# Attention scores of the second layer: computed once with queries on partitions, instead of twice

## The chip, the cores and the metric

The program runs on one core of a Trainium2 chip, in one launch. The metric is the device time of one execution in microseconds. The kernel before was run 23 times: median 2198.99 us, 2188.61 to 2218.9. All intermediate data stay on the device; the host only lays inputs out.

## The reference, cut to what matters

The model is two post-norm layers on 16 sequences of 512 tokens of width 128. Each layer is an attention and a mixture of experts. The change lies in the second attention, which has 16 heads of 8 dimensions and a bias that depends on the distance of query and key alone:

```python
rel = abs(r[None, :] - r[:, None]) / max(S - 1, 1)
idx = clip(round(rel * (RES - 1)), 0, RES - 1)
pos_bias = einsum('ijf,hf->hij', table[idx], Wpos)
q, k, v = split(einsum('bsd,ed->bse', x, Wqkv), 3)      # 16 heads of 8
logits = einsum('bihd,bjhd->bhij', q, k) * scale + pos_bias[None]
attn = softmax(logits, axis=-1)
out = einsum('bhij,bjhd->bihd', attn, v)
return einsum('bsd,ed->bse', out, Wout)
# around it: x = layernorm(x + first_attention(x)); x = layernorm(x + experts(x))
#            x = layernorm(x + this(x));            x = layernorm(x + swiglu_experts(x))
```

The softmax runs over the keys j. A stable softmax takes the row maximum over j from the logits of each query i before the exponential.

## The kernel before, in words

**Order of the work.** The program is written as a list of operations. Each has an engine, a cost, a due time, the buffers that it reads and writes, and a function that emits its instructions. The order in which they are emitted is a table of ranks, `ORDER`, one pair of characters for each operation, made ahead of time. It fixes the order of the instructions on each engine, with SP's transfers and POOL's among them. A tile framework adds the waits. At run time each engine takes its queue in that order, and stands when an operand or a buffer is not ready.

**Buffers.** Pools rotate. The ones that matter: `pair`, three PSUM buffers of 128 x 1024 f32; `one`, two PSUM buffers of 128 x 512 f32; `wide`, twelve SBUF buffers of 128 x 1024 f32. `pair` and `one` together are all of PSUM, and the other stages (the first attention, the experts) draw from the same pools.

**Stages.** The 16 sequences go through in chunks of 2, 3, 4, 3, 3 and 1. While a chunk is in its second layer, the next chunk is in its first, and the experts of the last one run too; the order mixes them closely.

**The second attention of one sequence** (`attention1`). Queries and keys are projected (L1208, L1209) and split into a rounded part `hi` and a rest `lo`, so that four products of rounded numbers make one exact enough score. They go through DRAM (`parts`, L1248) to be spread over partitions (`spread`, L1285). The 16 heads are taken in four groups of four; of a group the four tiles of 128 tokens are taken in turn, and heads in two pairs. For every group there are two passes over the scores:

- *The maxima* (`maxima`). A second copy of queries and keys, rounded to bf16, goes its own way through DRAM (`rounds`, L1259, and four small transfers a group into `qk16_pad`, L1272). For a tile of 128 queries and a pair of heads TensorE adds the bias into PSUM by a product with a bf16 identity (L1308) and the rounded scores on top (L1317): queries on partitions, 512 keys along the row. ScalarE casts the result to bf16 in SBUF (L1333). VectorE folds halves and quarters of the rows by maximum (L1349, L1365, L1376), reduces the rest (L1377) and keeps the negated maximum of each query in `tops`. TensorE turns `tops` (L1392), ScalarE copies it (L1400), and a transfer puts it as one more row beside the queries (L1405, `shift`). The maximum needs no exactness, since it only shifts the exponent.
- *The weights* (`weighted`). For a tile of 128 keys and a pair of heads TensorE forms the scores the other way round (L1422): keys on partitions, 512 queries along the row, with the shift row taken in by a key row of ones (L1858 sets it). VectorE adds the bias out of PSUM (L1441), ScalarE takes the exponential of 1024 columns at once (L1447). The result has keys on partitions, as the product with the values needs it: TensorE adds the four heads' values, weighted, into 4 x 32 rows of `av` (L1456), over the four key tiles. A ninth column of ones in `vaug` gives the sum of the weights.

`normalised` copies `av` (L1467), turns it (L1471) and divides (L1477, L1478). The maxima of a group are due 1.5 tiles before the weights of the group before it (`EARLY`).

The other lines that the prediction uses: L1073, where the first attention turns a tile of 128 x 1024 in eight transposes, and L1076, which copies it to SBUF; L1050, the running sums of the first attention; L1062, L1524, L1234, sums and products on VectorE that read PSUM; L618 and L620, the statistics of a layer norm; L636, its scaling on ScalarE with a scale and a bias of each row; L1143, the experts' activation with a bias of each row; L1223, a scaled copy out of PSUM.

Of the kernel before, what the change touches and what calls it, by code (L numbers as in the profile page):

```python
# [19 lines left out]
P = 128  # L20
# [34 lines left out]
    "#$###M#O#)#N#<#'#(#/#2#6#%#*#3#9#:#5#.#7#?#G#1#,#A#B#H#=#>#T#U#V#W#Y#@#-#P#R#X#4#&#S#b#l#;#+#_#j"  # L55
    "#m#8#Q#d#h#k#`#n#p#q#u#v#z#|#f#K#t$2$:#x#y%]$5$K#e#C#E#F#g#J#0&1%c#D#{$%#L#[#]#^#~$#$$#c#o$)$($0"
    "$*$,$/$4$=$D#i$&$-$6$9$;$<$>$?$H$I$a$1$3$B$C$F$M$G$N$S$T$g$l$@$A$O$P$W$[$]$^$_$o$t$u%-%.%2%7%Y%j"
    "#a#w#I$L$Q$R$U$Y$b$V$X$e$Z$c$f$p$v$z${%($`$d$q$s$y$~$|$}%$%*%4%@$w$x%#%&%'%3%/%1%8%9%I%L%%%)%0%:"
    "%;%=%>%B%C%M%N%S%Z%_%`%d%h%l%m%o%p%s%t&-&_&d'D&C&:&E&N&Q&V&`&b'K&T&m&X&^&x&}'$'*'b&R'9'1'2'?'@'N"
    "'U'd'H'a'W'_'n'o'u'v'w'~(8(:(<(>)*)A)Q)r+A#Z#r#s#}$'$+$.$7$m$8$i$h&'&%&G'](]$J$E%a&&'[$j%W%e$k&D"  # L60
    "'R0b.S)k%Q(A(B(O(V(F(P(H(I(G(Q({(x(c(Z(R([(t(b(q)c)$)s)H)E)F)K(d)-)0)O)1)2)7),).)4)U)>)@)C)D)I)L"
    ")[)l)()))/):);)=)V*'*(*5*:*<(w(_(u(v)g(z(|)#*X*P*T*b*Y*l*|)R)W)X)`)d)i)m*v*[*]*z*}+(+1)Y)e)f)8)?"
    ")G*%*w*o*p*y*x+'+@)M)S)T)5)6)<)n***r*~+$+-*u+<+E)|*)*/*#*$*,*C*D*F*K*f+#+L+M+R)_)b)a)h+H+7+9+U+D"
    "+C+O+Y+J+P+i*4*7*>)q)u)v*H+=+N+T+W+B+k+s*6*8*E)y)z){*U+?+c+g+r+G+I+t*;*=*?*2*3*9*I*L+0+d+l+|+3+j"
    ",%)})~*+*.*0*1*_*c*d*{+:+X,&,/,C*@*M*-*A,++o,,,6,*+Z+_+u,1,2,;*O*S*W*i*j*n+)+m+q+x,-+n+v,>*Z*^*e"
    "*a*g*h+5+^+w+{,:+y,$,B*k*q*s+%+&+*+++>+z,#,5,9+~,),H+.+4+;+,+2+6+F+Q+[+f+p,.,L,V,Z,P,<,?,b,Q,R,m"
    ",E,J,O,l,N,d,w,f,S,T,U,i,|,~,],[,g,o,c-#-'-,-8->-G-H-V-`-n-u.3.G.H.m/3.M.q.W.Y.u/</=9u,',(,e,k,0"
    ",4,@,3,=,M,A,^,D-D,F,a,W,X,G-j-X-0-]---.-2-+-/-4-@,{-&-),z-$-(-?-7-<-=,p,v,x-A-B,y,}-%,j,q,u-C-E"
    "-b.+.-.>,s-3-1,`-g-Z,n-h.A.C.E.K.D.I.V-L-Q-R-9-:-;-o.B.J.O.].P.a.c-a-d-s-I-M-O-t.Q.b.f.v.[.j.y-J"
    "-T-U-c-e-f-q-y.k.h.i.r.l/4/C-Y-[-_-w-{-}-~.&.4.;.R.T/F/V/b-S-^-W-5/(/*/#/'.z/G/O/^.~/_/g.*...2-k"  # L70
    "-z.#.{/A/J/R/i/I/N/l.7.<.?.%.5.:.n/P/Z/`/q/S/d/r.s.t.x.p.w.}/,/-/h/c/k/u/v/y0$.Z.`.g.^._.e.o/2/9"
    "/E/U/]0(0508./.0.=/)0&0+/n0%/p/z0)0//{020N.|/%/1/.///6/>0.0'000<040B0R/&/0/8/Y/a/e/m/~060E0F0*0;"
    "0`/7/;/?/:/@/D/Q/f0G0J0O0^0K0T0f/H/T/[/j/o/t/|0-010@0A0C0i0t0v0Q0M0P0Z0U0[0j0X0V0W0l0Y0h1$0g0c0k"
    "0~0m0p1%0q0r0u1#0s0w1&1'1*1+1217181>1?1B1H1J1Z1d1j1_1b1e1f1i2q3$;v$n$r%+%,%5%6%<%?%A%D%E%H%T%J%K"
    "%P%^%n&#%F%G%O%U%V%g%b%k%v%x&*&+%R%X%i%q%r%|%u%y&)&0&2&7%}%~&$&(&4&5&8&;&<&>&F&O&z'X'x'y(9(;'6%["
    "%f%w%z%{&.&/&9&,&3&A&6&?&@&H&I&]&q'&&=&B&L&M&W&Y&Z&a&c&h&o&y&J&P&S&[&k&l&r&s&t'#'3';&j&n&p&w&|'%"
    "''')','5'<'='O()(3(7(f(m&U&K&e&f&g&i&{&~&u&v'.'('8'-'/'0'4'I'Q'+'7':'A'B'E'M'P'S'^'`'k'>'C'F'G'V"
    "'g'Z'c'l'm'|(0'T'Y'e'q'z(#($(&(.(1(2(E(J(S(e(g(k(n(~)%)3)9)o)w)x,7,K,r*`+/*m*t+K+S+`+a/M+8+h+b+e"
    ",8,I,Y,h-K-*-6-F-N-i-|.6.9/$+}.F.(.)/5/B/W/X09-P/s/w/x0,030?0H0L0S0x0y1.1/0|1l1n4*4a1:2*2M4&4:1k"
    "2%2'2)1v2#2$2P2h2x3=3>3S3T3Y3]3Z3`3c3m3u9j3G4)44464@4D4A4J4N4^4b7X4S585f5l5u6s5~6+6y7d7m9X4Q8.7q"  # L80
    "7t9b9p9e9i9s:*:.:g;g=C=E?;?IFdI`;j<q=D>0>[?@At/+10112_3&13191<1@1;1F1T1U1[1`1R1S1o1x232m3F3#1g2I"
    "2N2b2<2?2@3'2=2>2J2224272{2E2K2L2Q2V2X3(332Y2Z2[2d2j2t2|34353:3O3P1X1Y1V1W262T2z3e3b3^3h3k3l3p4'"
    "2&2-201q1r1u2C4-3r3y4.4/41482A2B2F1c1p1s2G3i43494E3n4=4F1z1{1|2+21252D2e424;4B4K474H4T292:2;2.2/"
    "282H2f2g3[3_3d4X4_4d2^2]2y2l4<4O4R4>4Z3q3v3w4[4f4j2s2u3%2}2~3)374C4%4(4]4L4W4z2i2p2v3/383@3A4e4U"
    "4c4r4k4t4~3-3.32393B3C3I3J4o4h4u5$4q4w5+2w3*3,30313;3H3K3L3z4,4V5.50542R2U2S2O4x5#4p4y4`4{5'5(4g"
    "4s5:2`2a2c2n2o2r364n4}53595%5)5B3M3N3R3<3V3W3j525,5-565;5?5H3f3g3o3Q3U3X3t3|5&555A5D5*575J3~4#4+"
    "3x3}4$404G4I4i4m4|5K5W5b5I5@5N5Q5M5k5z5T5C5F5t5^5m5{5y5w5x6*5}6,6?5V6$6)6L5_5j6[6]6g6x7#7+7B7C7G"
    "7L7n7x889c9n8:8A8>8H8L8T8];t5>5G6/6B5L5S5P5Z5O5p5h6%64665[6&5`616'7?6~7,7K6N6S6V6D6G6K6k636>6A6-"
    "6<6=6I6X6c6e6R6T6U6z7%6C6F6J6@6E6M6h7&7'7Z7a7r6#625]656Q8C6:678,7w7{83868J8S6u6v6{6m6p6t727~7z8&"
    "8*8'818g6o6q6r6a6f6i7-8N8M8U8Z8R8Y8k7(7*7.6w7)757T7U8d8W8X8w8e8h8}787;7D7$70767E7^7o8$8+8?9%9.97"  # L90
    "6|717/6}9l9k9;9o8P8i8q8u8[8s9,7A7H7O77797:7P8j8o8v9(8n9&9/7b7c7e7F7I7J7f9*8x8y8z929S9_7h7s7y7l7v"
    "7}8)8-8r949@9Y8~9>9`7R7[7j7]7_7`7k80939M9T9t9d9~:&7@7>7<7=9h9m9G9F9w9v9z:$9|:6:C8=8E8K7Q7W7Y8Q:;"
    "9}:(:+:<:G:K9=9H9I9<9E9K9N9{:/:7:9:,:>:L9'9+9-8|9)95969A:I:0:4:Q:J:S:i9O9[9a9L9R9]:#:-:8:@:F:N:u"
    ";1;H:X:U:W:f:Y:`:{:q:Z:^:_:s:t;*:l:|;$;):o:p;8:h;#;(;.:n:};9;<;K;c;d;q<$<%<5<><B<C<J<Z<f<t=#<z=&"
    "='=:=A>.:1:2:V:a:3:::A:O:=:H:B:k:T:c:b:r:~:j;&;l;{;y;B;A;E;J;';+;,;m;/;7;@;-;5;>;b;L;M;R;O;Y;];n"
    ";o;4;6;:;f;s;}<-<6<8<D<I<M:m;W:d:e<e;w;V;P<v<T<]<|<w<}=5;S;X;a;T;U;`;r<x=3=7=9<{=2=Q<#<'<.;?;D;I"
    "<7=/=;=@=U=0=X=p;e;p;|<A<E<L<Q<_=6=<===J=8=?=v<&<)<1</<2<<<X<`<a=*=-=N>&>/>4;Z;u;z;x>(>)=M=O=q=^"
    "=`=|=w=z>1<[<g<h<Y<c<d<l=R=t=x>%=S=c>G<O<S<U<P<R<V<j=s=y={>@>$>D>H<=<G<K=$=)=,=F=G=j>9>:>F=r>+>I"
    "<+<3<;<:<@<F=(=V=f=u=}>,>J>f>g<s<u<r<b>c>;>b>?>P>E>O>e>T>h>n=T=Y=Z=L=P=W=e>B>X>Y>k>C>}>~=>=B=H=g"
    "=l=n>3>r>`>a?&>w?$?*=i=k=o=]=a=d>*>M>K>m>o>t>U>|?+=~>8>A>5>6>>>L>N>Q>^>i>j?2?8?:>v>y>{?/?'?.?3>p"  # L100
    "?0?7?B>q?1?K?)?4?<?G?5?H?L>x?6?9?F?,?J?M?N?S?T?W?X?Y?Z?[?]?c?d?e?f?g?h?~?q?r@)@1@SIf'J'L'f'h'i'j"
    "'p's'r't'{'}(((%(/(4(6(?(K('(*(+(,(@(C(L(M(N(U(s(}(=(D(X(Y(^(r(h(i(l)&)p*G(W(a(j)')J)P)^+V+]-m-v"
    "-x.8.@.L.U.X.d6;(-(5(T(`(o(p)B)N(y)+)t)Z)j)]*&*B*N*R*V,_,t-l-p.$.'.,.N/}0#0I0d*J*Q-r/K0]0a0_0e0z"
    "1)1=1M0=0D0n0o1,15161C1D1P1Q1]1^1t2W2k3+3D/L.1070:0>0{1(1-0}141A1I1K1N1a1h1m3a3s1E1G1L1O1}2,1~2("
    "454?5X5d1w1y3?3{5/5=5<5U5c5g6H6O4M4Y4l5R5a5i5o5q5s6W6j6n84898<8B8G8O4P3E4v515E5Y5e5v5n5r5|6(6.68"
    "6P6Y6Z73746^6_6b6l7M7V7N7S7g7p82856`6d7|8/878;8@8V8_8`8m8t8%8(8D8I8^8b8c8l8p8{9#9$90999:9?9B9C9D"
    "9U9V9^9r:E:R:x9y<y=1;C;=;N;[;~<*<4<9<n;2<?<,<0<k<m<~=%>-<i=4=+=.=I=K=[=_>'<p=b=h=m>#>7><>=>_>2>]"
    ">W>Z>l>s>u>z?->V?#?%?(?=?C?D?E?P?R?a?b?k?m?x@,@]AEC&BiD_EOGFG~CwDRH{J0KB?i?l?w@3?j?n@&A-?oA.@%A@"
    "Ah@BB%B,BNB]B[BbBtC$C/C2B}C@C<CIC^CyCcCpD,D@DAJ%C6G)EtEvGKGbGLGOGeGzH'MmD;H?GnGxHjI,HnHzI-JsJ|L#"
    "F>MDJSJfM_N$M`MbN,N4NPNQN|O2O`OjOkP$Q1P<VwVxWBX*ZXb|QPRbRiUcV#VcY<>d?p?t@$@*?u?z?{?v?y@'@5@V@-@X"  # L110
    "@+@U@N@7@9@pA6@oA#@`@b@d@Z@[@c@e@m@n@{A%A&A)A+@w@zA$@g@j@kA0A1@}A(A*A2A3A7A9A=A>ARAjAx@2@4@8@=Aw"
    "A[@lAyB&A|A~B5B(B8BG@?@@@H@a@f@h@iB;A}B#B9BHBMBU?O@6@C@J@K@P@RB>B6B<BKBABOBV@0@<@E@F@O@^@s@tBIBD"
    "BEBFBLBQBX@D@G@I@L@M@W@Y@u@vAJAoA{B`BeBnA/A,A5A4B{B|B~B^BRB.B7BCBSBWBoB)B+B-B/B1B4B=BTBfBkBlBaBh"
    "BvB$B'B*AeAgAsB2BcBgBqBwBdBmC4AlAmAnA]A^AaB?BJBxBzC%C'C(C+C8AfAiAkAqArAzB3BPBZBrBsC#C:C?CN@y@q@r"
    "@xC*C3C-C1CAC.C7CKCECMCVA:A;A<@|@~A'AUC0CCCDCOC>CGCWAHAKAQAPASAWAYC)CPCXCbC9CHC|ADAGAOA8AAACAVAX"
    "CSC[CjCtCTCUD4AMANATABAFAIAZA_A`B@BBCBDFDVDfD0C{C}D=D1D9DICYD#D&D(CZCgDLDKD'D.D/DSDUDiD:D<DCDMD?"
    "D^DkDmD{D~E'E+E8E:E;EAE]E_EpF&F6F9FUFDFJFVG,G;I&C]C`E0E1CaCfCdChClCqC~DOD7D8CmCnD$D+D6DZDbEDEID>"
    "DEDGDdDgDhDvDXD]DcD[D`DaDeDpDrDuDjDnDoDwDxDBDHDQDDDJDTE)E*E/E=EEEJDYD3D%DPFKDNDWDlEYEVEWE`EZEaF-"
    "E<E?E@D|E(E,EMF,F)F*F+F/F7F:E3E6E7E$E-E.EREfF.F2F=EgF1FEEBEFESE4E5E>ETEwF0FHFRFSF3FQFeEKENEUDqDy"
# [156 lines left out]
def block_kernel(ctx: ExitStack, tc: tile.TileContext, d, out: bass.AP):  # L276
# [900 lines left out]
    def attention1(b, x, at):  # L1177
# [117 lines left out]
        def maxima(g, it, lows):  # L1295
# [60 lines left out]
            if it < 2:  # L1356
                return
# [647 lines left out]
```

## Time and profile before

| | |
|---|---|
| median of 23 runs | 2198.99 us |
| profiled execution | 2203.36 us |
| its span, first to last instruction | 2201.6 us |
| mean granted TensorE clock | 0.961 of full speed |
| busy share of DMA engines, 320 to 2110 us | 0.35 |
| TensorE, VectorE, ScalarE busy, 320 to 2110 us | 1632.5, 1442.4, 1337.1 of 1790 us |

The prediction quotes lines of four kinds. A line of a group has the source line, the engine (PE is TensorE, PEld its weight loads, DVE VectorE, ACT ScalarE, POOL GpSimd, SP the queue of transfers), what is written from what, the shapes and the count; after the bar the time during which one of the group ran, the mean length of one in ns, and after the second bar the idle time of the engine just before them with what ended most of it. A line of the timeline has the start, the length and the operation, with neighbours of a kind merged. A line of waits has who waited for whom, the total, the times and the longest. Matmuls overlap, so a mean length says little of what one more costs.

### The profile page before, as it was taken

Reading aid. Unit: us, or ns where it says so; the run is one execution under the profiler, and the core shown is the slowest. Engines: PE = TensorE matmul, PEld = TensorE weight load, DVE = VectorE, ACT = ScalarE, POOL = GpSimd, SP = SyncE. Lnnn points to the kernel's source line nnn. Section 1 sums busy time; section 2 is a strip of 40 time slices with the busy share of each in tenths; the row PEclk is TensorE's granted clock in tenths of the full one; section 3 lists DMA queues with packets and bytes.
Section 4 is the critical chain, followed back from the end, with each engine's and each line's share of the span. In section 5 each row is a group of like instructions: output and inputs, shape, how many; then the busy total and the mean of one; then the engine's idle time right before and its main releaser. Section 6 shows DMA issues by size and latency. Waiting matters only on the chain. (4 is left out here: it accounts for less than half of the span.)

```text
span 2201.6 us, 32021 instructions
## 1 busy us (share of the span) xinstructions
PE 1957.7 (89%) x11336; PEld 1047.8 (48%) x11437; DVE 1694.5 (77%) x2894; ACT 1496.6 (68%) x2066; POOL 802.6 (36%) x879
## 2 busy tenths in 40 slices
PE   4878899998999898889999998899999799899887
PEld 1555644454455454344545443456455344443365
DVE  7555578797979686878797697979878787878866
ACT  5222468876776676667687788666677678799653
POOL 4335551244222634521333343442422633140343
PEclk9899999999999999989999999999999989999899
DMA  4416143423321442422233523233244434342343
GB/s 116 115 60 178 53 145 109 146 78 113 98 92 56 140 129 92 131 78 81 71 104 100 171 80 113 66 126 89 78 128 140 143 100 143 124 129 90 92 160 107
DMA packets 188579, 240.09 MB, mean 109 GB/s; under 512 B 22148, under 2 KB 132612, under 8 KB 188420
## 3 DMA queue, kind: packets, MB, share of 16 engines
q1 hardware_dynamic: 162868, 149.36, 22.5%
q0 software_dynamic: 25552, 88.68, 13.3%
q8 instruction: 91, 1.49, 0.3%
q14 instruction: 68, 0.56, 0.1%
HBM read 164.50 MB, written 80.42 MB: 111 GB/s over the span
## 5 line engine op out<-in xcount | busy, mean ns | idle before, releaser
L1441 DVE TENSOR_TENSOR p<-st,bias 128x1024 f32<-128x1024 f32 x512 | 606.1, 1218 | 81.4 <-PE st L1422 50.5
L1333 ACT CAST low<-s 128x1024 bf16<-128x1024 f32 x512 | 497.8, 1018 | 148.0 <-PE s L1317 114.1
L1447 ACT ACTIVATE p<-p 128x1024 f32<-128x1024 f32 x512 | 520.3, 1057 | 89.2 <-DVE p L1441 78.7
L796 POOL DMA_INDIRECT ws<-tab,rows x201 | 203.3, 1012 | 419.7 <-DVE yq L1153 172.0
L1308 PE MATMUL s<-bias,ident 128*128 128x512 bf16 x923 | 294.1, 400 | 45.1 <-ACT low L1333 26.5
L1456 PE MATMUL av<-p,vaug 128*32 128x512 f32 x2048 | 272.2, 610 | 5.4 <-ACT p L1447 2.7
L1422 PE MATMUL st<-qk_pad 64*128 64x512 f32 x1024 | 233.5, 490 | 47.4 <-DVE p L1441 22.4
L1034 POOL TENSOR_TENSOR self<-ev,own 128x1024 f32<-128x1024 f32 x64 | 127.0, 1986 | 336.2 <-DVE ev L1028 107.2
L1349 DVE TENSOR_TENSOR low<-low 128x1024 bf16<-128x1024 bf16 x256 | 182.7, 720 | 60.9 <-ACT low L1333 52.1
L1422 PEld LDWEIGHTS st<-qk_pad 64*128 64x128 f32 x1024 | 92.2, 189 | 228.6 <-DVE p L1441 71.7
L1308 PEld LDWEIGHTS <-ident 128*128 128x128 bf16 x1024 | 85.7, 99 | 194.0 <-issue 168.1
L796 POOL DMA_INDIRECT yg<-results,place x124 | 124.4, 1003 | 113.8 <-DMA results<-yq 51.1
L1317 PE MATMUL s<-qk_pad 32*128 32x512 bf16 x1024 | 154.7, 393 | 5.2 <-issue 5.1
L1050 PE MATMUL cum<-ev,tri 128*128 128x512 f32 x256 | 131.9, 641 | 16.1 <-DMA ev<-carry 12.5
L1076 ACT COPY ot<-po 128x1024 f32<-128x1024 f32 x64 | 64.8, 1013 | 111.3 <-PE po L1073 78.5
L1062 DVE TENSOR_TENSOR o<-cum,gg 128x1024 f32<-128x1024 f32 x64 | 78.3, 1223 | 79.5 <-PE cum L1050 36.8
L1081 PE MATMUL y<-ow,ot 128*128 128x128 f32 x1024 | 130.6, 283 | 2.7 <-ACT ot L1076 2.5
L1081 PEld LDWEIGHTS y<-ow,ot 128*128 128x128 f32 x1024 | 123.1, 196 | 18.4 <-issue 12.8
L1015 PE MATMUL pv<-vw,xt 128*128 128x512 f32 x256 | 126.2, 619 | 2.6 <-ACT carry L1057 1.5
L626 POOL TENSOR_SCALAR rs<-mv 128x4 f32<-128x4 f32 x63 | 22.0, 349 | 280.2 <-DVE mv L620 256.2
L1028 DVE TENSOR_TENSOR ev<-pv,ex 128x1024 f32<-128x1024 f32 x64 | 78.2, 1221 | 46.1 <-PE pv L1015 45.8
L1317 PEld LDWEIGHTS <-qk_pad 32*128 32x128 bf16 x1024 | 36.0, 91 | 154.7 <-issue 151.0
(226 smaller groups left out, 3173.9 us busy)
## 6 DMA issues: line engine op xcount, KB each, us to landing
qk_pad<-parts SPq DMA_DIRECT2D x256, 128.0 KB
parts<-lo SPq DMA_DIRECT2D x32, 512.0 KB
parts<-hi SPq DMA_DIRECT2D x32, 512.0 KB
xq<-tokens SPq DMA_DIRECT2D x42, 256.0 KB
results<-yq SPq DMA_DIRECT2D x42, 256.0 KB
bias<-rows SPq DMA_DIRECT2D x16, 448.0 KB
x<-in_x SPq DMA_DIRECT2D x16, 256.0 KB
xt<-in_xt SPq DMA_DIRECT2D x16, 256.0 KB
```

The source lines that it names most:

```text
L796: nc.gpsimd.indirect_dma_start(out, bass.IndirectOffsetOnAxis(to, 0) if to is not None else None, in_, bass.IndirectOffsetOnAxis(of, 0) if ...
L1034: lambda: nc.gpsimd.tensor_tensor(split(self_), split(ev), heads(own(), t), ALU.mult),
L1050: nc.tensor.matmul(cum()[:, hf, :], tri, ev()[:, hf, :], start=True, stop=True)
L1081: nc.tensor.matmul(y()[:, :P], ot()[:, hf, col(c)], ow[:, 4 * hf + c, :], start=(hf == 0 and c == 0), stop=(hf == 1 and c == 3),)
L1308: nc.tensor.matmul(s()[:, i, :], ident16, bias16[:, 4 * g + 2 * jp + i, 2 * u + 1 : 2 * (u + N) : 2], start=True, stop=False,)
L1317: nc.tensor.matmul(s()[:, i, :], pad[r, 0, col(it)], pad[r, 1, :], start=False, stop=True,)
L1333: lambda s=s, jp=jp, low=low: nc.scalar.copy(low().bitcast(BF16).rearrange("p i (j n) -> p (i j) n", j=2)[:, 2 * jp : 2 * jp + 2, :], s(),),
L1349: nc.vector.tensor_tensor(to[:, :, h * (it // 2) : h * (it // 2) + h], v[:, :, :h], v[:, :, h:], ALU.max)
L1422: nc.tensor.matmul(s[jp]()[:, i, :], pad[r, 1, jp, col(jt)], pad[r, 0, jp, :], start=True, stop=True,)
L1441: lambda jp=jp, h=h, pj=pj: nc.vector.tensor_tensor(pj(), s[jp](), bias[:, h : h + 2, u : u + N], ALU.add),
L1447: ACT, 1.0, lambda pj=pj: nc.scalar.activation(pj(), pj(), AF.Exp),
L1456: nc.tensor.matmul(acc()[32 * j : 32 * j + 32, :], va[:, jt, h * VW : h * VW + 32], p[j // 2]()[:, j % 2, :], start=(jt == 0), stop=(jt == ...
```

## The change

The scores are computed once, with queries on partitions. `maxima`, the bf16 copies (`low`, `rounds`, `qk16_pad`), `tops`, `shifted` and the row of ones go. `spread` moves the split queries and keys of a group in two transfers instead of four. For a tile of 128 queries and a pair of heads, TensorE forms the scores from 32 rows; VectorE adds the bias and takes the minimum of the negated row in one operation for each head, and writes the negated scores to SBUF; ScalarE takes the exponential for each head, with the minimum as a bias of each row; TensorE turns the weights, eight transposes into PSUM; ScalarE copies them to SBUF, and VectorE does for one of eight copies. When two tiles of queries are there, the values are summed for both: sixteen products of 256 columns. `wide` has nine buffers instead of twelve, three larger ones (`turned`) hold the turned weights. `ORDER` is new throughout.

```diff
-        "wide": (wp, [P, 2, N], F32, 12),
+        "wide": (wp, [P, 2, N], F32, 9),
+        "turned": (wp, [P, 4, N], F32, 3),
-        "mx": (wp, [P, P], F32R, 2),
+        "mx": (sm, [P, 2], F32, 4),
...
         def spread(g):
-            for j in range(4):
...
-            for i in range(2):
-                for k in range(2):
...
+            for k in range(2):
+                def move(k=k):
+                    nc.sync.dma_start(
+                        qk_pad[g % 2].bitcast(F32)[:, k, :],
+                        parts[b % 2][k, 32 * g : 32 * g + 32].rearrange("r c n -> (r c) n"),
+                    )
...
-        def maxima(g, it, lows):
...
-        def shifted(g):
...
-        def weighted(g, jt, acc):
+        def weighted(g, it, held):
             u = (NT - 1 - it) * P
+            pad = qk_pad[g % 2]
+            if it % 2 == 0:
+                held[:] = [buf("turned", f"pt_{b}_{g}_{it}_{jp}") for jp in range(2)]
             for jp in range(2):
+                h = 4 * g + 2 * jp
...
+                def scores(s=s, jp=jp):
+                    for i in range(2):
+                        r = slice(64 * jp + 32 * i, 64 * jp + 32 * i + 32)
+                        nc.tensor.matmul(
+                            s()[:, i, :], pad[r, 0, col(it)], pad[r, 1, :], start=True, stop=True
+                        )
...
+                def biased(s=s, p=p, low=low, h=h):
+                    for i in range(2):
+                        nc.vector.tensor_tensor_reduce(
+                            p()[:, i, :], s()[:, i, :], bias[:, h + i, u : u + N], -1.0, 3.0e38,
+                            ALU.add, ALU.min, low()[:, i : i + 1],
+                        )
...
+                def raised(p=p, low=low):
+                    for i in range(2):
+                        nc.scalar.activation(
+                            p()[:, i, :], p()[:, i, :], AF.Exp, bias=low()[:, i : i + 1],
+                            scale=-1.0,
+                        )
...
+                def turn(p=p, pt=pt):
+                    for i in range(2):
+                        for kt in range(NT):
+                            nc.tensor.transpose(pt()[:, i, col(kt)], p()[:, i, col(kt)], ident)
...
+                def kept(copy, pt=pt, to=to):
+                    copy(
+                        to().rearrange("p a (b u q) -> p (a b) u q", u=2, q=P)[:, :, it % 2, :],
+                        pt().rearrange("p i (k q) -> p (i k) q", q=P),
+                    )
+                if jp and it == NT - 1:
...
+        def summed(g, it, acc, held):
+            pts = list(held)
+            def values():
+                for kt in range(NT):
+                    for j in (2, 3, 0, 1):
+                        h = 4 * g + j
+                        w = pts[j // 2]().rearrange("p (i a) (b n) -> p i (a b) n", i=2, n=2 * P)
+                        nc.tensor.matmul(
+                            acc()[32 * j : 32 * j + 32, (it - 1) * P : (it + 1) * P],
+                            va[:, kt, h * VW : h * VW + 32], w[:, j % 2, kt, :],
+                            start=(kt == 0), stop=(kt == NT - 1),
+                        )
...
         for g in range(NG):
+            plan.due = at + NT * (g - 1) - EARLY
+            spread(g)
+            acc, held = buf("one", f"av_{b}_{g}"), []
             for t in range(NT):
                 plan.due = at + NT * g + t
-                weighted(g, t, acc)
...
+                weighted(g, t, held)
+                if t % 2:
+                    summed(g, t, acc, held)
             normalised(g, acc)
```

## The prediction

> **What bounds the kernel now.** I read the busy shares first, then the costliest groups, then the same groups one engine at a time, then the timeline of TensorE, and last the table of waits.
>
> ```profile
> span 2201.6 us, 32021 instructions
> PE 1957.7 (89%) x11336; PEld 1047.8 (48%) x11437; DVE 1694.5 (77%) x2894; ACT 1496.6 (68%) x2066; POOL 802.6 (36%) x879
> ```
>
> TensorE is the bound: 244 us of the span are left to it, 67 of them before 150 us and after 2100 us, where the attention in question hardly runs. VectorE and ScalarE have 507 and 705 us free. The groups that the change touches (first figure after the bar: busy us, second: mean ns):
>
> ```profile
> L1441 DVE TENSOR_TENSOR p<-st,bias 128x1024 f32<-128x1024 f32 x512 | 606.1, 1218 | 81.4 <-PE st L1422 50.5
> L1333 ACT CAST low<-s 128x1024 bf16<-128x1024 f32 x512 | 497.8, 1018 | 148.0 <-PE s L1317 114.1
> L1447 ACT ACTIVATE p<-p 128x1024 f32<-128x1024 f32 x512 | 520.3, 1057 | 89.2 <-DVE p L1441 78.7
> L1308 PE MATMUL s<-bias,ident 128*128 128x512 bf16 x923 | 294.1, 400 | 45.1 <-ACT low L1333 26.5
> L1456 PE MATMUL av<-p,vaug 128*32 128x512 f32 x2048 | 272.2, 610 | 5.4 <-ACT p L1447 2.7
> L1422 PE MATMUL st<-qk_pad 64*128 64x512 f32 x1024 | 233.5, 490 | 47.4 <-DVE p L1441 22.4
> L1349 DVE TENSOR_TENSOR low<-low 128x1024 bf16<-128x1024 bf16 x256 | 182.7, 720 | 60.9 <-ACT low L1333 52.1
> L1317 PE MATMUL s<-qk_pad 32*128 32x512 bf16 x1024 | 154.7, 393 | 5.2 <-issue 5.1
> ```
>
> The mean of one instruction is not its price in a full queue, because the next one starts before its row ends. The timeline shows the price as the distance between starts (columns: start, length, operation):
>
> ```profile
> 707.52 1.92 PE L1456 MATMUL av<-p,vaug 128*32 128x512 f32 x16
> 709.37 1.60 PE L1686 MATMUL pg<-xqt,ws 128*128 128x128 f32 x12
> ...
> 764.54 1.04 PE L1073 MATMUL po<-ident,o 128*128 128x128 f32 x8
> 765.41 0.60 PE L650 MATMUL pt_o<-ident,o 128*128 128x128 f32 x4
> ...
> 1012.39 1.08 PE L1308 MATMUL s<-bias,ident 128*128 128x512 bf16 x4
> 1013.40 0.39 PE L1317 MATMUL s<-qk_pad 32*128 32x512 bf16 x4
> 1013.72 0.55 PE L1471 MATMUL av<-ident,us 128*128 128x128 f32 x3
> ```
>
> Eight f32 transposes cost 0.87, not 8 x 0.28; two value products 1.85; a pair of rounded-score tiles 1.33. I counted every group of the timeline only until the next one starts; these "spaced" prices are used below. On TensorE 1941 us come out, so the busy time is real occupancy.
>
> **TensorE, the part on the path.** Removed: L1308 and L1317, spaced 268 + 137 = 404 us, and the small transposes L1392, 13. Together 417.
>
> Added: 512 operations of eight transposes. The same shape is L1073: 0.87 at best (446 us in all), 0.98 on its average over the trace (63.0 us for 64; 504 in all). In the new order they stand in 333 runs; I take 0.95 for the first of a run and 0.87 for each of the other 179: 472.
>
> Values: 128 operations of sixteen 256-column products replace 256 of four 512-column ones (257 us spaced). As many columns pass as in two old ones back to back, 1.85 above: 237. Two cost 1.85 and one alone 1.00, so 0.15 is a start-up; if every group of four paid it, one would be 4 x (0.425 + 0.15) = 2.3, 294 in all. I take 237, -20; ends -20 and +37.
>
> Scores: still 1024 products of 512 columns, 32 rows deep instead of 64. A pair costs 0.43 alone, two pairs in a row 0.67 (L1422), but two 32-row pairs (L1317) 0.33, as one. If the new ones joined so, the order's 120 doubles and 31 triples would save 0.24 each, -36. Runs otherwise stay alike (158 singles against 187): at worst +15, for 35 more pairs at 0.43. I take -5, because L1422 is the row of the same type.
>
> Sum: -417 + 472 - 20 - 5 = +30 us; ends -27 and +139.
>
> **VectorE, beside it.** Removed, spaced: L1441 587, L1349 175, L1365 89, L1376 81, L1377 40: 972. Added: 1024 fused add-and-minimum operations over 512 columns, each followed by a small instruction that writes the minimum out (the instruction order lists both), and 64 copies at 1.18 (as L1062), 75. No row shows the fused one. An add of 512 columns out of PSUM is spaced 0.60 to 0.66 (L1234, L1524) and the smallest instructions 0.08 (L620): 0.68 at best. By the mean rows it is 0.684 + 0.155 = 0.84. The dearest case is an add and a reduction one after the other: the reduction of 512 columns (L1377) is spaced 0.60, so 1.28. I take 0.70: 717 + 75 - 972 = -180; ends -200 and +414.
>
> [...] The rows of this trace start before the former has ended: four statistics of 0.28 take 0.78 to the next start.
>
> **ScalarE, beside it.** Removed, spaced: L1333 483, L1447 502, L1400 12, the bf16 copies of queries and keys 16, L1858 2: 1015. Added: 448 copies at 0.95 (L1333, L1076): 425; 1024 exponentials of 512 columns with a bias per row. Rows of 512 columns are spaced 0.51 (L1223), with no such bias. L1143, with one, takes 0.255 for 128 columns; at the slope between 512 and 1024 columns (0.978 - 0.508 over 512) 384 more make 0.60. L636, with scale and bias per row, takes 0.396, so 0.75. I take 0.60: 614 + 425 - 1015 = +24; ends -70 and +178.
>
> [...]
>
> **Queues and waits.** The longest waits of TensorE, and of SP's DMA queue (total us, times, longest):
>
> ```profile
> PE s L1308 <- ACT low L1333: 26.5, 45, 3.2
> PE st L1422 <- DVE p L1441: 22.4, 30, 4.4
> ...
> SPq L1405 <- ACT mx L1400: 303.7, 42, 22.4
> SPq L1285 <- PE st L1422: 298.5, 32, 22.5
> ```
>
> SP loses 465 issues (906 to 441 in its order: 256 L1272, 64 L1405, 16 L1259, half of L1285, one constant) and with them the 303.7 us in which it stood behind the shift L1405, other transfers behind it. I cost that at nothing: TensorE waits for qk_pad nowhere among its long waits, and the transfers that it does wait for (carry 12.5, ws 5.6) are POOL's. POOL loses four memsets. The order is a whole new one, so nothing keeps its neighbours.
>
> The waits on L1333 and L1441 are waits for a PSUM slot. Of the three "pair" slots, one of scores is now held 1.40 after its product instead of 1.13, and a transposed one is filled for 0.92 instead of 0.79 and held about as before: 0.4 more in 512 pairs, 205 slot-us, 68 over three slots. New waits: the transposes stand behind the exponentials in TensorE's queue, and what is queued there (products of the other block) waits too. Against that VectorE is 180 lighter, and the accumulator av takes one of two "one" slots only from the second tile on. I take -15 for VectorE's relief, +10 for the slots; ends: -60 (half of the 123 us before L1308, L1422, L1073 and L1050) and +60 (L1308's and L1422's again).
>
> **Sum.** The profiled execution took 2203.4: 2201.6 of span and 1.8 around it. 2203.4 + 30 - 15 + 10 = 2228. It stands 4.4 above the median of the runs, 2199.0; against the median I forecast 2224, 1.1% slower. Within 0.2% (2194.6 to 2203.4) is about what a measurement here can't tell from no change.
>
> **Rivals.**
> - *The idle time comes back (faster).* VectorE's 180 us and the freer accumulator slot take the full -60, transposes run at 0.87 and scores join: -27 - 60 gives 2112 at the end of both, 2150 to 2165 when half to two thirds are had. For it: 123 of 222 us of waits sit in front of four groups. Against: ScalarE, which holds the first of them, gets no lighter. It decides from the point where waits fall by more than TensorE's work grows, 30.
> - *ScalarE's split exponentials cost what L636 does.* +178 there instead of +24; ScalarE stands between the scores and the transposes, and reaches 1496.6 + 178 = 1675, 76%, VectorE's share now. If 60 of the 154 reach TensorE, 2284.
> - *The fused operation runs in two passes.* VectorE 1694.5 + 414 = 2109: at TensorE's present share of the span, 89%, that is 2370. [...]
> - *Values pay the start-up each time.* +57 over the sum: 2281. Against: PEld has half of the span free.
>
> **How the numbers follow.** Forecast 0.47 (own range 2185 to 2265), idle time back 0.31, ScalarE or values dearer 0.15, two passes 0.07. Below 2194.6 lie nearly all of the second and a little of the first: faster 0.34. Same 0.06, slower 0.60. The range from 2135 to 2320 leaves out the far end of the second case and the two-pass case, together under 0.2.
>
> **What would show it.** TensorE's busy time near 1990 and its share near 90%; transposes spaced 0.87 to 0.98 an operation; the fused operation and its small follower 0.70 together, VectorE near 1510; exponentials 0.60, ScalarE near 1520; waits of the transposes on the exponentials in place of L1308's on L1333. It is wrong if TensorE's idle time moves by more than 50 either way, or a fused operation is over 0.85.

## The result, and the profile after

The changed kernel takes 2258.5 us, the kernel before 2197.2: the ratio is 1.027, with an interval of [1.025, 1.030]. It is slower by 61 us, where the prediction said 25. The direction was right and the size was not, and the experiments show that the measured difference is a sum of large parts with opposite signs.

The page of the changed kernel (its profiled execution took 2263.5 us): span, busy shares, and the groups that answer to those shown of before.

```profile
span 2261.7 us, 41118 instructions
...
PE 2010.9 (89%) x15469; PEld 1457.9 (64%) x15469; DVE 1440.8 (64%) x3917; ACT 1546.5 (68%) x2416; POOL 763.1 (34%) x875
...
L1249 DVE CUSTOM_DVE_ANT_0 p<-s,bias 128x512 f32<-128x512 f32 x1024 | 651.9, 687 | 309.9 <-PE s L1238 175.3
L1260 ACT ACTIVATE p<-p,low 128x512 f32<-128x512 f32 x1024 | 670.1, 726 | 50.9 <-DVE low L1249 49.6
L1270 PE MATMUL tp<-ident,p 128*128 128x128 f32 x4096 | 540.3, 282 | 50.6 <-ACT pt L1275 18.4
...
L1275 ACT COPY pt<-tp 128x1024 f32<-128x1024 f32 x448 | 445.6, 1018 | 154.4 <-PE tp L1270 110.0
...
L1299 PE MATMUL av<-pt,vaug 128*32 128x256 f32 x4096 | 259.5, 393 | 7.2 <-DVE pt L1275 3.8
L1238 PE MATMUL s<-qk_pad 32*128 32x512 f32 x1024 | 204.1, 503 | 42.6 <-ACT pt L1275 19.1
```

TensorE's busy time rises by 53 us (1957.7 to 2010.9). What is left of the span beside it rises from 243.9 to 250.8. VectorE loses 254 us and ScalarE gains 50. The idle time ahead of the touched groups of TensorE (the figure after the second bar) was 107.9 us for the removed ones on record (45.1 + 5.4 + 47.4 + 5.2 + 4.8, L1308 to L1392), and is 100.4 here (50.6 + 7.2 + 42.6): so what VectorE gave up seemed to have bought nothing.

The waits of TensorE in the same execution (total us, times, longest):

```profile
PE s L1238 <- ACT pt L1275: 19.1, 28, 4.3
PE tp L1270 <- ACT pt L1275: 18.4, 25, 2.7
PE tp L1270 <- DVE low L1249: 16.8, 15, 4.3
...
PE tp L1270 <- issue: 8.6, 14, 1.7
```

In the last line TensorE is idle in the middle of a tile's transposes, waiting for nothing that the profile shows. It turned out to belong to the main thing.

**The kernels were timed in several sittings, and the sign depends on the sitting.** A sitting is a batch of kernels timed together, with the kernel before among them. Inside a sitting the runs of a kernel agree within 1%; between sittings the kernel before itself differs by 1.5%:

```
sitting            kernel before    changed kernel   ratio and interval
result, e1 to e4   2197.2, 2195.0   2258.5           1.027 [1.025, 1.030]
e5 to e8           2163.4           not run
e9 to e12          2192.7           2255.2           1.028 [1.025, 1.031]
e13 to e16         2166.8           2114.8           0.977 [0.974, 0.980]
e17, e18           2164.5           not run
```

The first row joins the sitting of the result and that of e1 to e4, whose kernel before differs by 0.1%. In the sittings of the first and the third row (call them the stopping ones, for what their traces show further down) the change costs 2.7 to 2.8%. In another, of the other kind, the same program gains 2.3%. The chip doesn't separate the kinds: by the record's chip numbers, e1 to e4 and e5 to e8 ran on the same one. All comparisons below stay within one row of this table, or say that they don't.

### The profile page after: what moved, and what is told of

Its sections match the earlier page's. It is cut to its first block, busy times and chain, and to the rows that moved or that the text cites. A ratio compares the mean times of both kernels' runs of the same rounds, so it can differ in the third digit from the quotient of the medians.

```text
span 2261.7 us, 41118 instructions
## 1 busy us (share of the span) xinstructions
PE 2010.9 (89%) x15469; PEld 1457.9 (64%) x15469; DVE 1440.8 (64%) x3917; ACT 1546.5 (68%) x2416; POOL 763.1 (34%) x875
## 5 line engine op out<-in xcount | busy, mean ns | idle before, releaser
L1249 DVE CUSTOM_DVE_ANT_0 p<-s,bias 128x512 f32<-128x512 f32 x1024 | 651.9, 687 | 309.9 <-PE s L1238 175.3
L1260 ACT ACTIVATE p<-p,low 128x512 f32<-128x512 f32 x1024 | 670.1, 726 | 50.9 <-DVE low L1249 49.6
L1270 PE MATMUL tp<-ident,p 128*128 128x128 f32 x4096 | 540.3, 282 | 50.6 <-ACT pt L1275 18.4
L1270 PEld LDWEIGHTS tp<-ident,p 128*128 128x128 f32 x4096 | 470.0, 145 | 127.3 <-issue 45.5
L1275 ACT COPY pt<-tp 128x1024 f32<-128x1024 f32 x448 | 445.6, 1018 | 154.4 <-PE tp L1270 110.0
L1299 PE MATMUL av<-pt,vaug 128*32 128x256 f32 x4096 | 259.5, 393 | 7.2 <-DVE pt L1275 3.8
L1238 PE MATMUL s<-qk_pad 32*128 32x512 f32 x1024 | 204.1, 503 | 42.6 <-ACT pt L1275 19.1
L1299 PEld LDWEIGHTS av<-pt,vaug 128*32 128x32 f32 x4096 | 124.2, 112 | 112.9 <-issue 39.6
L1238 PEld LDWEIGHTS s<-qk_pad 32*128 32x128 f32 x1024 | 78.6, 185 | 149.8 <-issue 43.1
L884 PE MATMUL py<-ws,h 128*128 128x128 f32 x804 | 104.1, 284 | 0.2 <-DVE h L1380 0.2
```

The costliest lines, as they stand in the source:

```text
L884: nc.tensor.matmul(py()[:, col(s)], h()[:, c, col(s)], ws[s]()[:, off + c * W : off + (c + 1) * W], start=(c == 0), stop=(c == 1),)
L1238: nc.tensor.matmul(s()[:, i, :], pad[r, 0, col(it)], pad[r, 1, :], start=True, stop=True)
L1249: nc.vector.tensor_tensor_reduce(p()[:, i, :], s()[:, i, :], bias[:, h + i, u : u + N], -1.0, 3.0e38, ALU.add, ALU.min, low()[:, i : i + 1],)
L1260: nc.scalar.activation(p()[:, i, :], p()[:, i, :], AF.Exp, bias=low()[:, i : i + 1], scale=-1.0,)
L1270: nc.tensor.transpose(pt()[:, i, col(kt)], p()[:, i, col(kt)], ident)
L1275: copy(to().rearrange("p a (b u q) -> p (a b) u q", u=2, q=P)[:, :, it % 2, :], pt().rearrange("p i (k q) -> p (i k) q", q=P),)
```

## The experiments

At the outset there were two theories for the +61 us. W: TensorE's added work sets it. E: the other engines' hand-overs set it, the copies and exponentials on ScalarE above all. The edits below are shortened to the calls that change; three dots stand for what is left out.

### First sitting (stopping; kernel before 2195.0)

**e1: more copies on VectorE.** VectorE had 254 us less to do, so all copies of the second head pair went to it.

```
-                if jp and it == NT - 1:
+                if jp:
```

> The changed kernel with the copies of the turned weights for the second pair of heads all on VectorE (256 copies there instead of 64, 256 on ScalarE instead of 448). Theory W, the time is TensorE's work plus idle time that the load of no other engine sets: 2258 within 15. Rival E, TensorE's idle time comes from ScalarE, which empties the PSUM slots of the transposes late: ScalarE is about 175 us lighter (192 copies at 0.91), VectorE 219 heavier but still under 1660, so 2180 to 2220.

Measured: 2338.8 us, ratio 1.068 [1.063, 1.073], 80 us above the changed kernel. VectorE gains 217 us of busy time, ScalarE loses 171, and what TensorE leaves of the span grows to 303 us (2339.0 - 2036.0). Neither number came. A copy on VectorE takes 1.22 us where ScalarE's takes 1.02, and TensorE's waits on VectorE double (73 to 145 us in all) while those on ScalarE fall from 105 to 83. VectorE's free time is not free at the moment it is wanted.

**e2: no minimum, no shift.** A plain addition over 1024 columns and one exponential for a tile; the softmax shift is left out.

```
-  for i in range(2): tensor_tensor_reduce(p[:, i], s[:, i], bias[...], ALU.add, ALU.min, low[:, i])
+  nc.vector.tensor_tensor(p(), s(), bias[:, h : h + 2, u : u + N], ALU.add)
...
-  for i in range(2): nc.scalar.activation(p[:, i], p[:, i], AF.Exp, bias=low[:, i], scale=-1.0)
+  nc.scalar.activation(p(), p(), AF.Exp)
```

> The changed kernel without the row minimum: a plain add of 1024 columns and one exponential of 1024 columns without a bias of each row, so that the softmax is not shifted (this part of the computation is left out). VectorE about 130 us lighter, ScalarE about 140 (512 times 1.24 down to 0.96), TensorE as before. Theory W: 2258 within 15. Rival E: 2180 to 2220. If both engines together matter and ScalarE alone does not, only this one of the two runs gets faster.

Measured: 2215.1 us, ratio 1.010 [1.005, 1.015], so 43 us below the changed kernel. Even without the minimum and the split the new shape isn't ahead of the kernel before in this sitting.

**e3: the kernel before with more work on TensorE.** 256 products like L1308 more, whose results the next product overwrites.

```
+                    if jp == 0:
+                        nc.tensor.matmul(s()[:, 0, :], ident16, bias16[...], start=True, stop=True)
```

> The kernel before with one bias product of 512 columns more for every first pair of heads (256 more, written over by the next, the values unchanged). At the spaced price of 0.22 to 0.27 that is 56 to 69 us more of TensorE work, about what the change adds (59). Theory W: 2250 to 2265, as slow as the changed kernel. Rival E: idle time takes up half or more of it, under 2230.

Measured: 2216.3 us, ratio 1.011 [1.006, 1.015]. TensorE's busy time rises by 35 us (1957.7 to 1992.9) and the time by 21: TensorE's work is worth some 0.6 of its busy time. By that slope the changed kernel's 53 us would make 32 of the 61. Counted from start to start, as the prediction does, the added products are 55 us (L1308's row goes from 265 to 321), and the slope is 0.4.

**e4: the weights turned as bf16.** The exponentials write bf16 and TensorE transposes bf16, so the weights lose accuracy.

```
...
-  nc.tensor.transpose(pt()[:, i, col(kt)], p()[:, i, col(kt)], ident)
+  nc.tensor.transpose(pt().bitcast(BF16)[...], p().bitcast(BF16)[...], ident16)
...
```

> The changed kernel with the weights written and turned in bf16 (the exponentials write bf16, the transposes are of bf16, the copies bring them back to f32; the rest unchanged, so that the weights are less exact). The transposes cost less: at 0.055 to 0.07 instead of 0.122 each, 215 to 275 us less of TensorE work. Theory W: 2258 minus most of that, 2010 to 2060. Rival E: the other engines, at 64 and 68 per cent now, and the slots hold it, 2110 to 2200.

Measured: 2230.2 us, ratio 1.017 [1.013, 1.021], 28 us below the changed kernel. The page's busy line:

```profile
PE 1869.5 (84%) x15469; PEld 1281.8 (57%) x15469; DVE 1438.6 (65%) x3918; ACT 1538.0 (69%) x2416; POOL 763.0 (34%) x875
```

141 us of TensorE's work are gone and 109 of them come back as idle time (250.8 to 360.0). W falls as the sole cause: taking work from TensorE gives a fifth of its busy time here.

### Second sitting (kernel before 2163.4)

The theories were now S (ScalarE's second exponential instruction for a tile is what costs) and V (VectorE's split fused operation is).

**e5: one exponential, fused additions kept.** The softmax shift is left out.

```
-  for i in range(2): nc.scalar.activation(p[:, i], p[:, i], AF.Exp, bias=low[:, i], scale=-1.0)
+  nc.scalar.activation(p(), p(), AF.Exp, scale=-1.0)
```

> The changed kernel with the fused add and minimum as it is, but one exponential of 1024 columns without a bias of each row (the shift of the softmax is left out). ScalarE about 140 us lighter, VectorE and TensorE unchanged. Leaving out both the minimum and the split took 2258 to 2215. Theory S, the split exponentials on ScalarE are the cost: 2215 to 2225. Theory V, the fused operation on VectorE is: 2245 to 2260.

**e6: plain addition, two exponentials.** The addition as in e2, the exponentials split with a bias of zeros; the shift is left out.

> The changed kernel with a plain add of 1024 columns and no minimum, and the two exponentials of 512 columns each with a bias of each row, read from a column of zeros (the shift of the softmax is left out). VectorE about 120 us lighter, ScalarE unchanged. Theory S: 2245 to 2260. Theory V: 2215 to 2225.

**e7: all 512 copies on ScalarE.**

```
-                if jp and it == NT - 1:
+                if False:
```

> The changed kernel with all 512 copies of the turned weights on ScalarE: 64 more there (about 58 us), 64 fewer on VectorE (75). Theory S, ScalarE's load is what is dear: 2268 to 2283. Theory Q, a copy in VectorE's queue stands until TensorE has turned the weights and holds up the adds behind it (192 more such copies cost 80): 2231 to 2245.

**e8: one shift for both heads of a pair.** One fused operation over 1024 columns with the minimum over both heads, one exponential with that bias. The softmax is the same, because any shift of a row cancels.

```
-  for i in range(2): tensor_tensor_reduce(p[:, i], s[:, i], bias[:, h + i, ...], ..., low[:, i : i + 1])
+  tensor_tensor_reduce(p(), s(), bias[:, h : h + 2, u : u + N], ..., low[:, 0:1])
...
+  nc.scalar.activation(p(), p(), AF.Exp, bias=low()[:, 0:1], scale=-1.0)
```

> The changed kernel with one fused operation over the 1024 columns of both heads, whose minimum is shared, and one exponential of 1024 columns with that one bias of each row. VectorE about 165 us lighter (512 times 0.08 + 1.13 against 1024 times 0.69), ScalarE about 125 (512 times 1.0 against 1.24). The weights are the same after the division. Theories S and V both: 2205 to 2225; if the bias of each row is dear in itself, not the split, ScalarE stays heavy and it is 2235 or more.

Measured: e5 2090.5 us, ratio 0.967 [0.965, 0.970]; e6 2129.5, 0.985 [0.983, 0.988]; e7 2162.0, 0.999 [0.998, 1.001]; e8 2099.1, 0.970 [0.968, 0.973]. Read against the changed kernel's 1.027, each of these edits seemed to gain 3 to 6%, even e7, which puts more work on ScalarE. e5 does more than e2 and stood 125 us below it. The ground had moved, and the kernel before showed it: 2163 instead of 2195.

### Third sitting (stopping; kernel before 2192.7): the same programs again

> The changed kernel itself, unaltered, beside three variants of it in one sitting, because the kernel before took 2195 us in the sitting of the first experiments and 2163 in that of the second, so that ratios of the two don't stand on one ground. Theory S (ScalarE's second exponential instruction for each tile is what costs): the ratio to the kernel before stays 1.02 to 1.03, and the two variants with one exponential for a tile are 60 us or more below it. Rival D (the sitting decides: what made the changed kernel slow is a difference of the whole chip, such as slower landings of transfers or a lower clock, that its order bears badly): the ratio goes to 0.98 to 1.00 here if the kernel before again takes about 2163, and the variants stand less than 40 us from it.

> The variant of e2 unaltered: plain addition, one exponential for a tile, no shift (the softmax shift is left out). It carries less work than the one-exponential and the plain-addition variants alone. S: 60 us or more below the changed kernel of this sitting, near the 2090 to 2130 that those two took in theirs if the kernel before takes 2163. D: it keeps its own ratio of 1.01, above those two though it does less on VectorE and ScalarE; then the order that its instructions fall into, and not the work, sets several per cent.

> The variant of e8 unaltered: one fused addition and minimum over both heads of a pair, one exponential with the shared minimum. S: 60 us or more below the changed kernel of this sitting, ratio to the kernel before 0.965 to 0.975 whatever that takes. D: ratio 0.99 to 1.01 if the kernel before is back near 2195.

**e12: e8 with all copies on ScalarE.**

> The variant of e8, and all 512 copies of the transposed weights on ScalarE (the 64 that VectorE had included). Moving those copies adds 64 x 0.94 = 60 us to ScalarE and takes 64 x 1.18 = 75 from VectorE. S: ScalarE is the dearer place, so 10 to 40 us slower than the variant of e8. Rival V (VectorE stands on the path as much): the same or up to 15 us faster. It is the version meant to be quickest, if V holds.

Measured: e9 (the changed kernel) 2255.2 us, ratio 1.028 [1.025, 1.031]; e10 (as e2) 2220.0, 1.011 [1.008, 1.015]; e11 (as e8) 2232.9, 1.017 [1.014, 1.020]; e12 2263.6, 1.030 [1.025, 1.035]. e8's program, instruction for instruction, took 2099 in one sitting and 2233 in the next. So S at its size of 60 us falls: on one ground a shared shift is worth 22 us and leaving the minimum out 35. The rest belongs to whatever separates the sittings.

### Fourth sitting (kernel before 2166.8): the changed kernel on the other ground

> The changed kernel, unaltered. If the kernel before takes 2190 to 2200 in this sitting: ratio 1.025 to 1.03 as in both others. If it takes about 2163: theory P (the places where TensorE stops are what makes the changed kernel lose): 2120 to 2140, ratio 0.98 to 0.99; rival W (its own work makes it lose): ratio 1.01 to 1.03, 2190 to 2225.

> The variant of e5 (fused additions with the minimum for each head, one exponential for a tile, no shift; the softmax shift is left out). In a slow sitting: 2220 + 13 (what the minimum cost between e10 and e11) = 2233 if the second exponential is what the split costs, so 22 below the changed kernel (S, now at the size that e9 and e11 leave it); level with the changed kernel if the split of the fused addition is what costs (V). In a quick one: 2090 again.

> The variant of e6 (plain addition, two exponentials, no shift; the softmax shift is left out). S: 2220 + 22 = 2242 in a slow sitting, near the changed kernel. V: 2220 to 2225, level with the variant that has neither. In a quick one: 2130 again.

> The variant of e7 (the changed kernel with all 512 copies of the transposed weights on ScalarE). In a slow sitting, as from e11 to e12: 31 us above the changed kernel, 2286. In a quick one: 2162 again. Rival: no dearer than the changed kernel, since VectorE loses 75 us.

Measured: e13 (the changed kernel) 2114.8 us, ratio 0.977 [0.974, 0.980]; e14 (as e5) 2091.2, 0.966 [0.962, 0.970]; e15 (as e6) 2129.7, 0.981 [0.978, 0.984]; e16 (as e7) 2162.7, 0.998 [0.997, 1.000]. P, as e13's expectation calls the theory of the stops, comes nearest: without them the change gains 52 us, a little more than P's range (2120 to 2140) allowed; W's 1.01 to 1.03 did not come. On this ground the parts can be priced. One exponential instead of two, the shift left out, saves 24 us, for 128 us less on ScalarE; TensorE's waits on ScalarE fall from 76 to 54 us. Moving 64 copies from VectorE to ScalarE costs 48, 0.75 for a copy of 1.02; TensorE's waits on ScalarE rise to 101, and its time at half clock from 90 to 135. So ScalarE is on the path, but its work has no one price: 0.19 of its length in the one edit, 0.75 in the other. Leaving the minimum out with the exponentials still split costs 15, although VectorE has less to do; why is open. TensorE's instructions stand in the same order in e10, e11, e13 to e16, so none of this is another order on TensorE.

The busy lines of the changed kernel in this sitting and, below, of the kernel before from e17:

```profile
span 2110.8 us, 41118 instructions
...
PE 1947.9 (92%) x15469; PEld 1418.8 (67%) x15469; DVE 1440.1 (68%) x3917; ACT 1539.4 (73%) x2416; POOL 761.8 (36%) x875
```

### Fifth sitting (kernel before 2164.5): the kernel before on the other ground

> The kernel before, unaltered, for a trace of this sitting beside the one on record (2203.4). In a quick sitting (2163 to 2167): no missing semaphore updates in the trace, TensorE's busy time 20 to 40 us lower than 1957.7 and its idle time lower, both where gathers are under way. In a slow one: 2190 to 2200, and stops as in the one on record.

**e18: the kernel before with 2048 more TensorE instructions for the same columns.** The score products of the weights (L1422) and the value products of the two middle tiles are issued in halves. The trace shows a value product as two instructions, so each kind adds 1024.

```
+  for c in range(2):
+      part = slice(2 * P * c, 2 * P * c + 2 * P)
       nc.tensor.matmul(s[jp]()[:, i, part], pad[r, 1, jp, col(jt)], pad[r, 0, jp, part], ...)
...
+  for c in range(1 if jt in (0, NT - 1) else 2):
       nc.tensor.matmul(acc()[32 * j : 32 * j + 32, part], va[...], p[j // 2]()[:, j % 2, part], ...)
```

> The kernel before, with 2048 more TensorE products for the same columns: each second score product in two halves of 256 columns (1024 more), and the value products of the two middle tiles in halves (1024 more). Work by spaced prices: 512 columns of values 0.125 in one and 2 x 0.061 in two, so 0 to +25 us in all. Theory N (what the stops cost goes by the number of TensorE instructions: 8165 more matmuls and loads gave 111 us more in the changed kernel, so 4096 more give 55): in a slow sitting +55 to +80 us, 2250 to 2275; in a quick one 0 to +25, 2165 to 2190. Rival O (it goes by something else of the changed kernel, such as which work its order puts beside the gathers): 0 to +25 in either.

Measured: e17 2165.5 us, ratio 0.999 [0.998, 1.001]; e18 2168.6, ratio 1.002 [1.000, 1.003]. In e17 TensorE's busy time is 16 us below that on record, where 20 to 40 was expected. Without stops, 2048 more instructions for the same columns cost 3 us, with an interval of 0 to 7: their number has next to no price there. The sitting was not a stopping one, so N (the stops' cost goes by that number) was not put to its test by e18. The busy lines of e17:

```profile
span 2166.1 us, 32021 instructions
...
PE 1941.4 (90%) x11336; PEld 1043.2 (48%) x11437; DVE 1696.0 (78%) x2894; ACT 1496.1 (69%) x2066; POOL 805.1 (37%) x879
```

### What the sittings differ in: two traces of one program

e9 and e13 are the same program, row for row, so a row's start in one trace can be set against its start in the other. The timeline of TensorE in e9 (columns: start, length, operation, idle time before):

```profile
934.52 1.06 PE L1270 MATMUL tp<-ident,p 128*128 128x128 f32 x8 [0.40 <-ACT p L1260]
935.42 0.38 PE L859 MATMUL pts<-ident,xq 128*128 128x128 f32 x2
936.15 0.27 PE L859 MATMUL pts<-ident,xq 128*128 128x128 f32 x1 [0.35 <-issue]
936.87 0.33 PE L859 MATMUL pts<-ident,xq 128*128 128x128 f32 x1 [0.45 <-issue]
941.44 1.94 PE L1270 MATMUL tp<-ident,p 128*128 128x128 f32 x8 [4.24 <-DVE low L1249]
943.17 3.02 PE L1519 MATMUL pg<-xqt,ws 128*128 128x128 f32 x16
```

The same rows in e13:

```profile
902.98 1.06 PE L1270 MATMUL tp<-ident,p 128*128 128x128 f32 x8 [0.39 <-ACT p L1260]
903.88 0.60 PE L859 MATMUL pts<-ident,xq 128*128 128x128 f32 x4
904.32 1.04 PE L1270 MATMUL tp<-ident,p 128*128 128x128 f32 x8
905.38 2.02 PE L1519 MATMUL pg<-xqt,ws 128*128 128x128 f32 x16
```

Four transposes of one operation, which need nothing new between them, take 0.60 us in e13 and come in pieces over 1.8 us in e9 (935.42 to 937.20). Then TensorE stands still for 4 us, and what follows runs at half pace (1.94 for eight transposes instead of 1.04), with the granted clock at 0.50 of full speed from 941 to 944 us. From the start of the first row to that of the last it is 2.4 us against 8.7. In the worst place, at 1806 us of e9, eight transposes take 4 us and TensorE, VectorE and ScalarE all stand for 7 to 10 us (6.7, 10.3 and 10.0), while GpSimd goes on for most of it: in the changed kernel's trace on record, which stops at the same rows, VectorE stands from 1806.3 to 1816.6 and a gather starts on GpSimd each 1.25 us, the last ending at 1814.0. What ends the idle time of the two others is shown as unknown (total us, times, longest; VectorE's waits of e9, then ScalarE's):

```profile
DVE p L1249 <- PE s L1238: 164.9, 123, 5.5
...
DVE p L1249 <- remote: 44.3, 8, 10.3
```

```profile
ACT pt L1275 <- remote: 33.0, 8, 11.5
ACT us L1314 <- remote: 17.0, 3, 10.0
```

"remote" on a one-core program means that no record of the trace accounts for the release. The trace of the changed kernel on record lacks 82 of 1848 semaphore updates by TensorE, 185 of 2631 by VectorE and 183 of 2126 by ScalarE; the kernel before on record lacks 7 to 10% too. The traces of e5, e8, e13 and e17 lack almost none, and show no such waits.

Where does the difference pile up? I cut the span after its first 60 us into stretches of 10 us and took the growth of the delay between the two traces in each, apart by whether the queue of GpSimd's gathers (software_dynamic on the page) had packets under way in it:

```
pair of traces                      growth us   stretches with gathers   without
changed, e13 and e9                 140         139.4 in 153             0.6 in 50
e8's program, e8 and e11            134         135.9 in 154             -2.3 in 48
before, e17 and the one on record   35.5        36.6 in 165              -1.1 in 44
```

All of it lies beside the gathers. In the changed kernel a stretch in which they fill over a tenth of the 16 engines' time loses 1.4 us, one in which they fill under a hundredth nothing. Transfers of the other large queue don't do it: 19 stretches in which those fill over 0.4 of the engines' time and gathers under a hundredth lose 0.1 us each. So the stops happen while GpSimd's gathers run, and they cost the changed kernel 141 us and the kernel before 35. Which engine stops first isn't shown, nor whether it is GpSimd's work on the gathers or their packets that matters. N, the rival that e18 could not test, is weakened by the same table cut again by TensorE's rate: at 110 to 140 TensorE instructions in 10 us, with gathers, a stretch of the kernel before loses 0.17 us and one of the changed kernel 0.85.

Two things stay open. One is what the stops are. Records are lost in the same sittings, and the timed runs agree with the profiled ones (e9: 2255.2 us by the median, 2255.3 profiled), so a common cause of both is possible, but nothing here shows it. The other open thing is why the changed kernel pays four times as much.

## Why the prediction was wrong

On the record the sum was 2203.4 + 30 - 15 + 10, and the measured parts are +53 for TensorE's busy time and +7 for what it leaves free. The step that failed is the one on waits: "I take -15 for VectorE's relief, +10 for the slots; ends: -60 ... and +60". It was wrong twice, in opposite directions: the waits that it prices fell by far more, and the stops, worth more than all its terms, stand in no term at all.

**Waits without stops: -62 instead of -5.** Between e17 and e13 what TensorE leaves of the span falls from 224.7 to 162.9 us. The idle time ahead of the touched groups goes from 94.6 (L1308, L1317, L1422, L1456, L1392) to 45.7:

```profile
L1308 PE MATMUL s<-bias,ident 128*128 128x512 bf16 x923 | 289.3, 394 | 35.0 <-ACT low L1333 18.4 <-DVE o L1062 4.5 <-DVE p L1441 3.8
L1456 PE MATMUL av<-p,vaug 128*32 128x512 f32 x2048 | 269.8, 607 | 5.3 <-ACT p L1447 2.8 <-issue 0.9 <-ACT mx L1400 0.6
L1422 PE MATMUL st<-qk_pad 64*128 64x512 f32 x1024 | 229.4, 483 | 41.9 <-DVE p L1441 21.7 <-ACT low L1333 8.9 <-ACT ot L1076 2.3
L1317 PE MATMUL s<-qk_pad 32*128 32x512 bf16 x1024 | 152.4, 389 | 5.4 <-issue 5.2 <-DVE o L1478 0.2
...
L1392 PE MATMUL pm<-ident,tops 128*16 128x128 f32 x64 | 17.9, 280 | 7.0 <-DVE tops L1377 6.0 <-DVE x L1089 0.5 <-DVE kept L1577 0.2
```

Those are groups of e17, and these of e13:

```profile
L1270 PE MATMUL tp<-ident,p 128*128 128x128 f32 x4096 | 517.7, 275 | 15.3 <-ACT pt L1275 6.7 <-DVE low L1249 2.7 <-ACT carry L1012 2.3
...
L1299 PE MATMUL av<-pt,vaug 128*32 128x256 f32 x4096 | 249.1, 382 | 3.6 <-DVE pt L1275 2.1 <-DVE l_m L1064 0.6 <-DVE cnt L736 0.4
L1238 PE MATMUL s<-qk_pad 32*128 32x512 f32 x1024 | 202.1, 492 | 26.8 <-ACT pt L1275 15.5 <-DVE low L1249 3.9 <-ACT h L1098 1.2
```

This is the rival "the idle time comes back", whose end was -60, and whose time of 2150 to 2165 is 0.978 to 0.985 of the median: 0.977 was measured. It was held down because ScalarE "gets no lighter". It got heavier by 43 us, and TensorE's waits on it shrank nevertheless, from 93 to 76 us. Those on VectorE fell by 31, from 78 to 47: the relief priced at -15 was twice that. The sign "waits of the transposes on the exponentials" did not come: in e13 they are 0.8 us, and the transposes wait for copies and fused operations.

**Stops: +141 for the changed kernel, +35 for the old, and no term for either.** The prediction looked at transfers only as something that TensorE waits for (carry 12.5, ws 5.6) and costed the rest at nothing. In the trace on record the hint was there, though only e17 beside it makes it one: "remote" behind idle time of VectorE and ScalarE (7.7 and 5.9 us; none in e17), "issue" ahead of TensorE's groups (19.9 us; 7.9 in e17), and DMA landings that the trace doesn't tell. The difference, 106 us by the traces and 115 by the medians of the third and fourth sitting, turns a gain of 52 into a loss of 62. Between e13 and the changed kernel's execution on record, again the same rows in the same order, the span differs by 151, and with that the sum closes: -55 without stops (e17 to e13), +151, -35.5, together the +60 between the two spans on record. That the sittings differ by this much, beside the gathers, is shown; what makes the stops come is open.

**TensorE's work: right in sum, in part by luck.** The term was +30. By spaced prices in e13 and e17 the touched groups give 480 for transposes, 239 - 254 for values, 183.5 - 209.6 for scores, less 410 removed: +29. Single terms: transposes 472 forecast, 480 without stops, 501 on record; values -20 against -15 and -9; scores -5 against -26 and -28, since the 32-row pairs did join more than L1422 let expect; the removed work 410 instead of 417. These errors, +8, +5, -21 and +7, cancel. The busy time itself differs from +30, and the clock can account for it: TensorE spent 137 us at half clock in e17 and 90 in e13, 173 and 235 on record. If half of that time is lost work, the busy difference at equal clock is 6.5 + 23.5 = 30 without stops and 53 - 31 = 22 on record, an estimate, since part of the half-clock time is idle. The prediction had no term for the clock either: without stops +30 of work, -23.5 of it and -62 of waits make the -55.

**VectorE: too careful.** -254 instead of -180. The timeline of e13 shows why:

```profile
1704.09 0.69 DVE L1249 CUSTOM_DVE_ANT_0 p<-s,bias 128x512 f32<-128x512 f32 x1
1704.70 0.09 DVE L1249 DVE_READ_ACCUMULATOR2_ANT low<- 128x1 f32 x1
1704.70 0.69 DVE L1249 CUSTOM_DVE_ANT_0 p<-s,bias 128x512 f32<-128x512 f32 x1
...
1705.31 0.08 DVE L1249 DVE_READ_ACCUMULATOR2_ANT low<- 128x1 f32 x1
1705.31 0.69 DVE L1249 CUSTOM_DVE_ANT_0 p<-s,bias 128x512 f32<-128x512 f32 x1
```

A fused operation with its accumulator read is spaced 0.61, not 0.70: the read ends inside the next operation's row. The two-pass rival is out. The count of two instructions holds: the changed kernel's trace on record has 1024 of the one (687 ns) and 1024 of the other (84 ns). The price by row means, 0.84 for the two and so -37 in all, does not.

**ScalarE: the price nearly right, its place wrong.** Split exponentials are spaced 0.63 on average (643 us for 1024 in e13), forecast 0.60; the mean of their rows on record, 0.726, is a row's length and not a spacing. The +24 became +43 to +50. "Beside it" was wrong: e16 pays 48 us for 64 copies more, though e14 gets back only 24 for 128 us less.

**Values paying a start-up** is out (239 us). The sign to watch for, "TensorE's idle time moves by more than 50 either way", came true without stops.

## A version that does better

e8 and e11 compute the whole reference with one fused operation and one exponential for a tile. Without stops that is 0.7% under the changed kernel (ratios 0.970 and 0.977), and with them 22 us under it (2232.9 against 2255.2 in one sitting). Against the kernel before it is 3.0% faster in one sitting and 1.7% slower in the other. Nothing that was run beats the kernel before in a stopping sitting.

## What to carry to other kernels

Run the kernel before in every sitting, and compare ratios across sittings only when it stays put: here a 1.5% shift of it went with a 6% shift of the changed kernel and turned the verdict over. "Remote" and "issue" ahead of rows that need nothing new can be the trace of a cost of its own (141 us of the changed kernel here), and a sum that leaves it out can have the wrong sign. Busy shares don't tell what an engine's work is worth: a copy added to ScalarE, free for 27% of the span, cost three quarters of its length, while of work taken away a fifth came back, from ScalarE (e14) as from the "bound" TensorE (e4).

## What the runs showed of the hardware that was not expected

- One program, 2099 us in one sitting and 2233 in another (e8, e11), with TensorE's rows in the same order; the whole difference in stretches where gathers are under way.
- An add with a row minimum (687 ns for 512 columns on record) and its accumulator read (84 ns) are spaced 0.61 us in e13, less than the operation's own row.
- Half-clock time moves with the stops: 90 us in e13 and 235 in the changed kernel on record, 137 in e17 and 173 in the kernel before on record, and 359 in e4, also with stops, where TensorE had least to do (1869.5 us busy).
